# Reordering the gate steps and the removal counts in the first part of a two-layer graph kernel

## The chip, the cores and the metric

The kernel runs on one core of one Trainium2 chip. The metric is the device time in microseconds (us) of one execution, as the median of several. Engines: PE is TensorE, DVE is VectorE, ACT is ScalarE, POOL is GpSimd, SP is SyncE, which here only issues transfers. PEld is TensorE's loading of weights.

## The reference, cut to what matters

There are 16 graphs of 1024 nodes with 128 channels. Layer 0 is a gated graph network with four rounds; layer 1 first thins the neighbour lists of the same adjacency ("dilation"), row by row, and then runs three aggregating layers.

```python
# layer 0: x = layernorm(x + gated(x, adj))
for i in range(4):
    m = einsum('bjn,bjd->bnd', adj, h @ weight[i])
    gx, gh = m @ w_ih.T + b_ih, h @ w_hh.T + b_hh
    r = sigmoid(xr + hr); z = sigmoid(xz + hz); n = tanh(xn + r * hn)
    h = (1 - z) * n + z * h

# layer 1 begins with, for each graph, rows in order:
def step(carry, n):
    row = carry[n]; num = sum(row)
    sf = where(num > 10, (num + 1) // 2, 1)
    rank = cumsum(row)
    rm = row & (rank % sf == 0)        # if num > 1
    carry[n] &= ~rm; carry[:, n] &= ~rm
# ... three aggregating layers, a linear layer, layernorm
```

Both the four gated rounds and the thinning need only the inputs. The kernel runs them side by side: this is its first part, and the only one the change touches.

## The kernel before

**Gated rounds.** Two graphs are worked on at a time, each by a "stream". A layer of one stream is 32 products of the adjacency with h (h split in a high and a low half of its bits, two halves f of 512 nodes, 8 blocks j), then for each half f four gate sums and the gate steps. `aside(n)` is a hook: it advances the thinning by one step and does small jobs for the other stream, so that they lie between the products. This is the order in which each engine's queue is filled[...].

```python
    def layer(self, st, l, aside):
        ...
        for f in range(2):
            for n, part in enumerate((st.hi, st.lo)):
                aside(2 * f + n)
                if l == 0 and f == 1 and n == 0:
                    st.begin(1)
                for j in range(NB):
                    nc.tensor.matmul(pm[f], part[:, j, :], st.adj[j][:, half[f]], ...)   # L1074
            m = wk.tile([C, HF], F32, name="h_ms")
            nc.scalar.copy(m, pm[f])                                                     # L1077
            ms.append(m)
        aside(4)
        ...
        for f in range(2):
            h, m = st.ht[:, half[f]], ms[f]
            ...
            pr = gate((w(self.wh, 0), h), (w(self.wi, 0), m))                            # gate: L1086
            nc.scalar.activation(r, pr, AF.Sigmoid, bias=bias(self.bs, 0))               # L1095
            aside(5 + 2 * f)
            ph = gate((w(self.wh, 2), h))
            nc.vector.scalar_tensor_tensor(r, ph, bias(self.bh, 2), r, ...)              # L1098
            px = gate((w(self.wi, 2), m))
            nc.vector.tensor_add(r, px, r)                                               # L1100
            nc.scalar.activation(r, r, AF.Tanh, bias=bias(self.bi, 2))                   # L1101
            aside("rest" if f == 0 else 8)
            pz = gate((w(self.wh, 1), h), (w(self.wi, 1), m))
            nc.scalar.activation(z, pz, AF.Sigmoid, bias=bias(self.bs, 1))               # L1104

            nc.gpsimd.tensor_tensor(zh, z, h, ALU.mult)                                  # L1106
            nc.vector.scalar_tensor_tensor(r, z, 1.0, r, op0=ALU.subtract, op1=ALU.mult) # L1107
            nc.gpsimd.tensor_tensor(h, zh, r, ALU.subtract)                              # L1108
            aside(6 if f == 0 else 9)
```

The hook. In mid-graph its jobs are the "turn" of the other stream's new h (four transposes on PE, L1025), the copy of its high part ("split", ACT, L1013), and the low part ("rest", DVE, L1018), once for each half of h; the other stream's next products need them. Where the other stream ends or begins a graph, its jobs are the ending and beginning instead.

```python
            jobs = {5: [lambda: ot.next_layer(0)], "rest": [lambda: ot.rest(0)],
                    7: [lambda: ot.next_layer(1)], 8: [lambda: ot.rest(1)]}
        ...
        def aside(n):
            if n not in ("rest", 8):
                next(steps, None)
            for job in jobs.get(n, ()):
                job()
            if n == 8:
                next(steps, None)
```

**Thinning.** A block is 128 rows of four graphs, and there are 32 blocks. A block takes 20 steps, that is two layers (10 hooks each that advance it). Cut to the order of the work:

```python
            yield; old.settle(); old.wide_u(0)        # the block before: third counts, its rows
            yield; old.wide_u(1); old.rows(0)
            ...                                       # rows(g): DVE L863; wide_u: ACT L909, L912
            for g in range(4):                        # spread over the steps
                self.turn(i, g)                       # PE L722
                self.keep(i, a[g])                    # DVE L727
                self.count(i, g, a[g], rank, pt)      # DVE L735, a running count along the row
            q = self.params(num, 0)                   # DVE, some seven ops on 128x4
            u = self.diag_u(rank[:, :, diag], q)      # ACT L886, four
            yield
            x = self.removed(u, q, both)              # DVE L893, four: the removal mask
            yield; yield
            pd, num = self.less(x, rank, 1)           # PE L901, four, then DVE L903: second counts
            q = self.params(num, 1, ...)              # DVE L694 to L701, with L818
            u = self.diag_u(rd, q)                    # ACT L886, four
            yield
            x = self.removed(u, q, both)              # DVE L893
            yield; old = self.Block(self, i, a, rank, both, x)
```

`settle` is the third and last round: it starts with `less` (PE L901, DVE L903) and params again. With the offset of the start, the second round's counts fall on `aside(7)` of the first stream's layer, the second removal on its `aside(8)`, and `settle` on `aside(1)` of the second stream's layer.

Of the kernel before, what the change touches and what calls it, by code (L numbers as in the profile page):

```python
# [15 lines left out]
ALU = mybir.AluOpType  # L16
# [9 lines left out]
NB = N // P  # L26
HF = 512
L0 = 4
# [888 lines left out]
class Gated:  # L917
# [24 lines left out]
    def bank(self):  # L942
        return self.ps6.tile([P, HF], F32, name="h_g")
# [117 lines left out]
    def layer(self, st, l, aside):  # L1061

        nc, wk = self.nc, self.wk
        half = [slice(f * HF, (f + 1) * HF) for f in range(2)]
        bank = self.bank
        pm = [bank() for f in range(2)]
        ms = []
        for f in range(2):
            for n, part in enumerate((st.hi, st.lo)):
                aside(2 * f + n)  # L1070
                if l == 0 and f == 1 and n == 0:
                    st.begin(1)
                for j in range(NB):
                    nc.tensor.matmul(pm[f], part[:, j, :], st.adj[j][:, half[f]],  # L1074
                                     start=(j == 0 and n == 0), stop=(j == NB - 1 and n == 1))
            m = wk.tile([C, HF], F32, name="h_ms")
# [3 lines that stand above are left out]
        bias = lambda t, g: t[:, 3 * l + g:3 * l + g + 1]  # L1080
        w = lambda t, g: t[:, l, g, :]

        def gate(*mm):
            pg = bank()
            for i, (lhs, rhs) in enumerate(mm):
                nc.tensor.matmul(pg, lhs, rhs, start=(i == 0), stop=(i == len(mm) - 1))  # L1086
            return pg

        for f in range(2):
            h, m = st.ht[:, half[f]], ms[f]  # L1090
            r = wk.tile([C, HF], F32, name="h_r")
            z = wk.tile([C, HF], F32, name="h_z")
            zh = wk.tile([C, HF], F32, name="h_zh")
            pr = gate((w(self.wh, 0), h), (w(self.wi, 0), m))
# [3 lines that stand above are left out]
            nc.vector.scalar_tensor_tensor(r, ph, bias(self.bh, 2), r, op0=ALU.add, op1=ALU.mult)  # L1098
# [4 lines that stand above are left out]
            pz = gate((w(self.wh, 1), h), (w(self.wi, 1), m))  # L1103
            nc.scalar.activation(z, pz, AF.Sigmoid, bias=bias(self.bs, 1))  # L1104

            nc.gpsimd.tensor_tensor(zh, z, h, ALU.mult)  # L1106
            nc.vector.scalar_tensor_tensor(r, z, 1.0, r, op0=ALU.subtract, op1=ALU.mult)  # L1107
            nc.gpsimd.tensor_tensor(h, zh, r, ALU.subtract)  # L1108
            aside(6 if f == 0 else 9)

    def run(self, steps):

# [27 lines left out]
    def beside(self, st, ot, l, s, b0, steps):  # L1140


        before = l if s == 0 else l + 1
        if before in (0, L0):
            old = not (s == 0 and b0 == 0)
            new = not (s == 1 and b0 + 2 >= B)
            jobs = {5: [], 7: [], 9: []}
            nxt = ot.b + 2 if old else ot.b

            def begin():  # L1150
                ot.b = nxt
                ot.begin(0)

            if old:
                jobs[5].append(lambda: ot.finish(0))
                jobs[7].append(lambda: ot.finish(1))
                jobs[0] = [lambda: ot.load_x(nxt)]
                for j in range(4, NB):
                    jobs.setdefault(j // 2 - 2, []).append(lambda j=j: ot.load_adj(nxt, j))
            if new:  # L1160
                jobs.setdefault(5 if old else 0, []).append(lambda: ot.begin_rows(nxt))
                jobs[9].append(begin)
        else:
            jobs = {5: [lambda: ot.next_layer(0)], "rest": [lambda: ot.rest(0)],
                    7: [lambda: ot.next_layer(1)], 8: [lambda: ot.rest(1)]}

        if l == L0 - 1:

            for j in range(4):
                jobs.setdefault(4, []).append(lambda j=j: st.load_adj(st.b + 2, j))  # L1170

        def aside(n):
            if n not in ("rest", 8):
                next(steps, None)
            for job in jobs.get(n, ()):
                job()
            if n == 8:
                next(steps, None)
        return aside

# [809 lines left out]
```

## Time and profile before

| what | value |
|---|---|
| time, median of 3 | 2517.11 us (2514.15 to 2519.67) |
| profiled execution | 2516.4 us, 35661 instructions |
| first part | about 40 to 1417 us: 64 layers, 32 blocks |
| PE, DVE, ACT, POOL busy, share of the span | 91%, 76%, 55%, 41% |

The page has the span in 40 equal slices; each digit is the busy share of a slice in tenths.

```
PE   6999999999999999999999599999999989988875
DVE  4888888888878878888888777777777466665667
ACT  3556455556455564556564456666666445545647
```

The first 22 slices are the first part. DVE is busier there than anywhere later, ACT about half busy. [...]

### The profile page before, as it was taken

What the parts mean: (1) busy time and instruction counts of PE and PEld (TensorE: products, weight loads), DVE (VectorE), ACT (ScalarE), POOL (GpSimd) and SP (SyncE); (2) the same over time, 40 slices, a digit from 0 to 9 for tenths busy, and PEclk for the clock granted to TensorE, in tenths of its full rate; (3) what the DMA queues carried; (4) which work ended last, traced back from release to release, by engine and by line L of the source; (5) the groups of instructions that cost most, each with busy time, mean ns of one, the idle gap of its engine ahead of it and who ended that gap; (6) DMA issues with size and microseconds to landing.
All of it is one profiled execution on the core that took longest, in us unless ns stands there. A gap on an engine that the chain in (4) does not pass through costs nothing.

```text
span 2516.4 us, 35661 instructions
## 1 busy us (share of the span) xinstructions
PE 2287.6 (91%) x11897; PEld 1574.4 (63%) x11913; DVE 1925.0 (76%) x4153; ACT 1390.1 (55%) x3228; POOL 1035.2 (41%) x937
## 2 busy tenths in 40 slices
PE   6999999999999999999999599999999989988875
PEld 4556555555555565555555377777777777777654
DVE  4888888888878878888888777777777466665667
ACT  3556455556455564556564456666666445545647
POOL 3335234253353352442532376666666244440000
PEclk9999999999999999999999899999999999999988
DMA  7327245263363272443631487787777366655304
GB/s 248 106 91 248 68 141 179 88 216 109 103 213 106 92 248 68 149 171 102 216 100 60 141 305 271 280 294 289 283 278 260 135 218 235 232 167 157 118 16 130
DMA packets 214389, 436.17 MB, mean 173 GB/s; under 512 B 59570, under 2 KB 80724, under 8 KB 214196
## 3 DMA queue, kind: packets, MB, share of 16 engines
q1 hardware_dynamic: 186756, 345.96, 39.8%
q0 software_dynamic: 23040, 83.90, 9.8%
q10 hardware_dynamic: 4400, 3.95, 0.5%
q8 instruction: 96, 1.57, 0.3%
q14 instruction: 97, 0.79, 0.1%
HBM read 324.49 MB, written 109.25 MB: 172 GB/s over the span
## 4 chain that ended last, share of the span: by engine, by line
PE 42%; DVE 32%; ACT 15%; issue 6%; DMA 4%; POOL 1%; SPq 0%; DVEq 0%; ACTq 0%; POOLq 0%
PE p_ag L1531 9%; PE h_g L1074 8%; PE h_g L1086 7%; DVE f_rank L735 7%; DVE f_x L893 3%; DVE h_r L1107 3%; ACT f_pd L886 2%; ACT s_junk L1368 2%; PE q_ag L1764 2%; PE p_u L1458 2%; PE p_u L1459 2%; PE p_u L1452 2%; DVE f_a L727 2%; DVE h_r L1100 2%; DVE h_r L1098 2%
## 5 line engine op out<-in xcount | busy, mean ns | idle before, releaser
L1106 POOL TENSOR_TENSOR h_zh<-h_z,h_h 128x512 f32<-128x512 f32 x128 | 203.9, 1593 | 501.3 <-ACT h_z L1104 501.0
L1086 PE MATMUL h_g<-h_h,h_wh 128*128 128x512 f32 x768 | 397.8, 600 | 0.0
L1086 PE MATMUL h_g<-h_ms,h_wi 128*128 128x512 f32 x768 | 392.2, 592 | 0.0
L1074 PE MATMUL h_g<-h_a,h_hi 128*128 128x512 f32 x1024 | 289.7, 422 | 48.2 <-ACT h_hi L1013 48.2
L1467 POOL CAST p_b<-p_at 128x512 uint8<-128x512 f32 x256 | 256.4, 1021 | 129.7 <-ACT p_at L1460 129.7
L735 DVE TENSOR_TENSOR_SCAN f_rank<-f_a,f_first,f_pd 128x1024 f16<-128x1024 f32 x128 | 299.2, 2343 | 3.0
L1074 PE MATMUL h_g<-h_a,h_lo 128*128 128x512 f32 x1024 | 272.0, 410 | 0.0
L1460 ACT ACTIVATE p_at<-p_u,s_less 128x512 fp32r<-128x512 f32 x256 | 175.7, 688 | 156.9 <-PE p_u L1459 140.4
L1086 PEld LDWEIGHTS h_g<-h_ms,h_wi 128*128 128x128 f32 x768 | 145.8, 190 | 183.8 <-issue 164.9
L1074 PEld LDWEIGHTS h_g<-h_a,h_hi 128*128 128x128 f32 x1024 | 188.3, 190 | 114.7 <-ACT h_hi L1013 58.6
L1074 PEld LDWEIGHTS h_g<-h_a,h_lo 128*128 128x128 f32 x1024 | 201.2, 200 | 42.1
L863 DVE SCALAR_TENSOR_TENSOR f_nr<-f_u,f_q,f_a 128x1024 bf16<-128x1024 f16 x128 | 164.0, 1284 | 77.4 <-ACT f_u L912 68.1
L1476 DVE SCALAR_TENSOR_TENSOR p_a<-p_a 128x1024 bf16<-128x1024 f32 x128 | 210.5, 1685 | 3.7 <-DMA p_a<-in_adj_dram 3.7
L1101 ACT ACTIVATE h_r<-h_r,h_bi 128x512 f32<-128x512 f32 x128 | 92.6, 723 | 181.8 <-DVE h_r L1100 181.6
L1368 ACT ACTIVATE s_junk<-s_o 128x128 bf16<-128x128 f32 x384 | 113.7, 298 | 129.1 <-DVE s_o L1361 129.1
L1086 PEld LDWEIGHTS h_g<-h_h,h_wh 128*128 128x128 f32 x768 | 129.2, 191 | 82.4 <-issue 66.3
L1107 DVE SCALAR_TENSOR_TENSOR h_r<-h_z,h_r 128x512 f32<-128x512 f32 x128 | 114.1, 891 | 86.6 <-ACT h_z L1104 86.3
L1108 POOL TENSOR_TENSOR h_h<-h_zh,h_r 128x512 f32<-128x512 f32 x128 | 163.9, 1281 | 27.9 <-DVE f_tr L903 17.2
L909 ACT ACTIVATE f_u<-f_rank,f_q 128x128 f16<-128x128 f16 (+7 forms) x128 | 110.5, 866 | 89.2 <-DVE f_rank L849 89.2
L1077 ACT COPY h_ms<-h_g 128x512 f32<-128x512 f32 x128 | 73.8, 577 | 152.6 <-PE h_g L1074 111.1
L1458 PE MATMUL p_u<-ident_b,p_a 128*128 128x128 bf16 x1024 | 145.0, 222 | 5.1 <-DMA p_a<-in_adj_dram 4.1
L1459 PE MATMUL p_u<-ident_b,p_nr 128*128 128x128 bf16 x1024 | 144.9, 222 | 0.0
(242 smaller groups left out, 4899.4 us busy)
## 6 DMA issues: line engine op xcount, KB each, us to landing
h_a<-in_adj_dram POOLq DMA_DIRECT2D x128, 512.0 KB, 7.2
p_a<-in_adj_dram SPq DMA_DIRECT2D x128, 512.0 KB
f_a<-in_adj_dram SPq DMA_DIRECT2D x124, 512.0 KB
e_nr<-f_nr SPq DMA_DIRECT2D x128, 256.0 KB
p_nr<-e_nr SPq DMA_DIRECT2D x32, 1024.0 KB
s_at<-p_b SPq DMA_DIRECT2D x32, 512.0 KB
s_ag<-s_ag SPq DMA_DIRECT2D x64, 256.0 KB
q_agi<-s_ag SPq DMA_DIRECT2D x32, 512.0 KB
```

The costliest lines, as they stand in the source:

```text
L735: nc.vector.tensor_tensor_scan(out, a, other[:, 0, 0:1].to_broadcast([P, N]), start, op0=ALU.add, op1=ALU.bypass)
L1074: nc.tensor.matmul(pm[f], part[:, j, :], st.adj[j][:, half[f]], start=(j == 0 and n == 0), stop=(j == NB - 1 and n == 1))
L1086: nc.tensor.matmul(pg, lhs, rhs, start=(i == 0), stop=(i == len(mm) - 1))
L1106: nc.gpsimd.tensor_tensor(zh, z, h, ALU.mult)
L1107: nc.vector.scalar_tensor_tensor(r, z, 1.0, r, op0=ALU.subtract, op1=ALU.mult)
L1368: self.nc.scalar.activation(junk, o[:, i, :], AF.Square, accum_out=ss[:, i:i + 1])
L1458: nc.tensor.matmul(pu[:, i * P:(i + 1) * P], a[:, blk, 1], ib, start=False, stop=False)
L1459: nc.tensor.matmul(pu[:, i * P:(i + 1) * P], nr[:, k, blk], ib, start=False, stop=(i == 3))
L1460: nc.scalar.activation(g["at"][:, j, cols], pu, AF.Relu, bias=self.less2)
L1467: self.nc.gpsimd.tensor_copy(g["b", f][:, j, :], g["at"][:, j, f * HF:(f + 1) * HF].bitcast(F32))
L1476: self.nc.vector.scalar_tensor_tensor(low, a, 0.0, a, op0=ALU.is_gt, op1=ALU.not_equal, accum_out=self.bad[:, c:c + 1])
L1531: self.nc.tensor.matmul(pa, hi[:, j, :], at[:, j, f * HF:(f + 1) * HF], start=(start and n == 0), stop=(stop and n == len(js) - 1))
```

## The change

Three things change in the order of instructions; none is added or left out.

1. In `aside(7)` of layers whose other stream is in mid-graph, the turn and split of h's second half come before the step of the thinning (second counts, their parameters, L886).
2. The last two gate steps of the first half (L1107 and L1108) are put off until both halves' gates are emitted. They thereby come behind the steps at `aside(7)` and `aside(8)`: the second counts and the second removal in the first stream's layer, the masking of row 1 in the second's. The second half's L1106 now stands behind the first half's L1108 on GpSimd.
3. `aside(1)`, with the third counts of the block before, moves from ahead of the low products of the first half to between the fourth and the fifth of them.

They are meant to let the products and the thinning wait less for each other. Lines of the changed kernel are up to 12 higher than those of before.

```diff
@@ layer: products
             for n, part in enumerate((st.hi, st.lo)):
-                aside(2 * f + n)
+                if (f, n) != (0, 1):
+                    aside(2 * f + n)
                 if l == 0 and f == 1 and n == 0:
                     st.begin(1)
                 for j in range(NB):
+                    if (f, n, j) == (0, 1, NB // 2):
+                        aside(1)
                     nc.tensor.matmul(pm[f], part[:, j, :], st.adj[j][:, half[f]],
@@ layer: gates
+        rest = []
         for f in range(2):
             h, m = st.ht[:, half[f]], ms[f]
...
             pz = gate((w(self.wh, 1), h), (w(self.wi, 1), m))
             nc.scalar.activation(z, pz, AF.Sigmoid, bias=bias(self.bs, 1))
 
-            nc.gpsimd.tensor_tensor(zh, z, h, ALU.mult)
+            rest.append((r, z, zh, h))
+            if f == 0:
+                nc.gpsimd.tensor_tensor(zh, z, h, ALU.mult)
+                aside(6)
+        for f, (r, z, zh, h) in enumerate(rest):
+            if f == 1:
+                nc.gpsimd.tensor_tensor(zh, z, h, ALU.mult)
             nc.vector.scalar_tensor_tensor(r, z, 1.0, r, op0=ALU.subtract, op1=ALU.mult)
             nc.gpsimd.tensor_tensor(h, zh, r, ALU.subtract)
-            aside(6 if f == 0 else 9)
+        aside(9)
@@ beside: the hook
         def aside(n):
-            if n not in ("rest", 8):
+
+            first = n == 7 and before not in (0, L0)
+            if not first and n not in ("rest", 8):
                 next(steps, None)
             for job in jobs.get(n, ()):
                 job()
-            if n == 8:
+            if first or n == 8:
                 next(steps, None)
         return aside
```

## The prediction

> **What bounds the kernel now.** I read the page's busy line first, then the busy times by stretch, then the waits of TensorE and VectorE in the first part, and last the timeline of one period.
>
> ```profile
> PE 2287.6 (91%) x11897; PEld 1574.4 (63%) x11913; DVE 1925.0 (76%) x4153; ACT 1390.1 (55%) x3228; POOL 1035.2 (41%) x937
> 40.00:1417.00 1377.00, 1292.27 (x5029) 786.42 (x5027) 1151.03 (x2214) 764.13 (x1410) 543.86 (x485) 0.98 0.41 136
> ```
>
> The second line is the first part, the only one that the change touches (span, then busy time of PE, PE loads, DVE, ACT, POOL). TensorE idles 1377.0 - 1292.3 = 84.7 us there. The part holds 64 gated layers, alternately of two streams. The row-removal search takes 20 steps for a block of rows and a layer calls 10, so layers pair up: in A (first stream) the search counts rows 2 and 3 and does its first and second removal, in B (second stream) it settles the third count, writes the rows and counts rows 0 and 1 of the next block. There are 32 pairs, of 1377/32 = 43.0 us.
>
> ```profile
> PE h_g L1074 <- ACT h_hi L1013: 48.2, 24, 2.1
> PE f_pd L901 <- DVE f_x L893: 32.8, 44, 1.9
> ```
>
> These two waits (total, times, longest) are 81.0 of the 84.7 us. The first is the product that wants the split of h's second half, once in each of the 24 pairs in which the other stream is in mid-graph; the second is a count of removals waiting for VectorE's removal mask.
>
> ```profile
> DVE h_r L1107 <- ACT h_z L1104: 86.3, 90, 2.9
> DVE f_nr L863 <- ACT f_u L912: 68.1, 92, 1.2
> ```
>
> VectorE, in turn, loses most of its waiting to L1107, the last gate step, which stands in its queue before its z is there. The timeline at the A-to-B seam shows what that does (start, duration, engine and line):
>
> ```profile
> 827.56 0.68 DVE L1018 TENSOR_TENSOR h_lo<-h_g,h_hi 128x512 fp32r<-128x512 f32 x1
> 829.00 0.69 DVE L1107 SCALAR_TENSOR_TENSOR h_r<-h_z,h_r 128x512 f32<-128x512 f32 x1 [0.77 <-ACT h_z L1104]
> 829.62 0.16 DVE L903 TENSOR_TENSOR f_tr<-f_rank,f_pd 128x4 f32<-128x4 f16 x1
> ...
> 831.06 1.95 ACT L886 ACTIVATE f_pd<-f_rd,f_q 128x128 f32<-128x128 f16 x4 [1.51 <-DVE f_t L700]
> 832.95 0.58 ACT L1013 CAST h_hi<-h_g 128x512 fp32r<-128x512 f32 x1
> 833.55 0.69 DVE L1018 TENSOR_TENSOR h_lo<-h_g,h_hi 128x512 fp32r<-128x512 f32 x1 [0.84 <-ACT h_hi L1013]
> 833.58 1.21 PE L1074 MATMUL h_g<-h_a,h_hi 128*128 128x512 f32 x4 [2.05 <-ACT h_hi L1013]
> 834.16 1.12 DVE L893 SCALAR_TENSOR_TENSOR f_x<-f_pd,f_q,f_both 128x128 bf16<-128x128 f32 x4
> 834.79 1.27 POOL L1106 TENSOR_TENSOR h_zh<-h_z,h_h 128x512 f32<-128x512 f32 x1 [2.61 <-ACT h_z L1104]
> 835.20 1.42 DVE L1107 SCALAR_TENSOR_TENSOR h_r<-h_z,h_r 128x512 f32<-128x512 f32 x1
> 835.34 0.40 PE L901 MATMUL f_pd<-f_tri,f_x 128*128 128x128 bf16 x4 [0.56 <-DVE f_x L893]
> 836.54 0.15 DVE L903 TENSOR_TENSOR f_tr<-f_rank,f_pd 128x4 f32<-128x4 f16 x1
> ```
>
> L1107 holds up the second round's parameters (L903 on); these hold up ScalarE's L886; L886 stands before the split (L1013) in ScalarE's queue; the split holds up the product and lo; lo holds up the mask; the mask the third count. The loop that sets the period is thus the search itself, on VectorE and ScalarE, round to the next block; TensorE waits where it meets it. That is my choice of bound, and it matters: shortening only TensorE's waits would move them elsewhere.
>
> [...] the split starts at 832.95, behind L886, though the turn it reads was issued at 826.46 and ran 0.61 us. [...] L1107 at 835.20 takes 1.42 us, ending 0.56 after GpSimd's L1106 ended at 836.06, against 0.69 undisturbed. [...] here six banks rotate, and in the built program the turn of the second half waits for the bank that the first half's r sigmoid reads. This bears on a rival below.
>
> **The change, part by part**, on the pair above. No instruction is added or dropped; only places in queues move. R is the end of L1100 of the first half in A, at 827.64.
>
> Turn before counts, and L1107 put off, in A. Lo of the first half ends at 828.24. L903 then follows at about 828.28 instead of 829.62, 1.34 earlier (0.77 of wait and 0.69 of work gone, less overlap). L700, whose end releases ScalarE, ends at 829.69 instead of 831.03. The second half's r sigmoid ends at 829.56 (828.88 + 0.68), and the split now follows it: 829.56 to 830.14. The product that waited needs it after four products, about 831.0: the 2.05 us wait is gone. L886 runs 830.1 to 832.05. Meanwhile VectorE does L1098, L1100 and lo of the second half, until about 832.0, and the mask (1.12) ends at 833.2 instead of 835.28: 2.06 earlier.
>
> Third count four products on. TensorE starts its products at 830.01, eight take about 1.9 us, four more 0.9: it reaches the count at 832.8, at the mask's arrival but for 0.4 us. Before, it would have stood still from 832.0. VectorE now does both L1107 (2 x 0.69), 833.2 to 834.6, and goes on with L903 at 834.6 instead of 836.54: 1.94 earlier.
>
> B. The rows (L863) are paced by ScalarE's L909/L912, which start 1.94 earlier too; the last row ends about 2.0 earlier. Then the block's own mask (L774), L1098, L1100 and lo as before; L1107 of the first half with its wait (0.77 + 0.69) no longer stands before row 0's masking and count, so these come 2.0 + 1.46 - 0.1 = 3.3 earlier. It comes back behind row 1's masking, with 0.69 and without the 0.31 us that the second half's L1107 waited there: 3.3 - 0.69 + 0.31 = 2.9 earlier from there to the next R.
>
> So the search's loop shortens by about 2.8 us a pair. In the eight pairs in which the turn is not moved (a graph ends or begins there), L1107 waited 2.90 us in the one at 744.15; there ScalarE becomes free for L886 only 2.1 earlier, and L903 of the settling gains about 1.9, so these gain as much. 32 x 2.8 = 90 us. TensorE cannot give that much: its idle time is 84.7 us in all, plus small holds inside runs of matmuls (a 0.50 us load wait at 827.70). On the pair above, 42.39 us from third count to third count (835.34 to 877.73), I take off its waits of 2.05, 0.56 and 0.26 and about 0.5 of load waits: 39.0 us of pure TensorE. The loop would come to 42.4 - 2.8 = 39.6. Two lengths so close do not interlock without loss; I keep 75%: 32 x 2.8 x 0.75 = 67 us. The end of the part costs about 1.5 us: after the last layer h's first half is ready only behind the second half's gates, and GpSimd does its three steps one after another (1.27 each). 2517 - 67 + 1.5, rounded down a little for the contention that L1107 loses (mean 891 ns against 690; 128 x 0.2 = 26 us of VectorE, a part on the loop): 2449 us.
>
> **Rivals.** (1) TensorE is the bound and its wait only moves, to the first round's count, where 16 pairs already wait 0.2 to 1.5 us for the mask. Against it: these masks come from the same loop, which is shortened. For it: if ScalarE rather than VectorE paced B, the 0.9 of gain in B would be lost, leaving 1.94 x 32 x 0.75 = 47 us: 2470. (2) GpSimd's three steps now run back to back after the mask, from 834.6 to about 838.4 (3 x 1.27), into the first row at 837.6, which reads two SBUF tiles and would stand still some 0.8 us. For it: the 1.42 us above. Against: later rows wait 0.6 us each for ScalarE, and swallow it. If they did not: 32 x 0.8 x 0.75 = 19 us less, 2468. (3) The turn, now ahead of the second round's count, waits for its bank: in the heavy pair at 1044 the r sigmoid ends at 1043.98 and the mask at 1044.60, so turn and count would fall together. The count would come up to 0.5 us later in perhaps 16 pairs: 6 to 8 us, 2456. (4) [...] granted 0.98 here; one point over the part would be 14 us.
>
> **Range and chances.** All three losses together would still leave some 25 us of gain; full interlock would give 80 to 90. I take 2430 to 2473 for 8 in 10. The line of 2% is 2466.8, which rivals 1 and 2 would each just miss: faster 0.77, same 0.22, slower 0.01.
>
> **What would show it.** Right: L1074's wait on L1013 gone from TensorE's list; L1107's wait on L1104 far under 86 us; the period from third count to third count near 40.9; TensorE's idle time in the part under 35 us. Rival 1: waits of L901 on L893 at the first round's count grow beyond 20 us. Rival 2: L863's mean rises above 1284 ns. Rival 3: the turn (L1025) appears waiting for L1095. I am wrong if the period shrinks by under 1.5 us, above all if row 0's count does not come about 3 us earlier after the seam.

## The result, and the profile after

The changed kernel takes 2426.2 us (median of five, 2424.7 to 2427.8) against 2517.0 us (2514.2 to 2519.7) for the kernel before: a ratio of 0.964, 95% interval 0.9627 to 0.9654. That is 91 us less. I had predicted 2449 us, 2430 to 2473: the direction was right, the gain was a third larger than said, and the result lies just below the range.

The busy line of the page after, and the busy times of the first part, which now ends near 1323 us instead of 1417 (span, then PE, PE loads, DVE, ACT, POOL, granted clock of TensorE, share of the DMA engines, GB/s):

```profile
PE 2260.7 (93%) x11897; PEld 1558.2 (64%) x11913; DVE 1927.9 (80%) x4153; ACT 1384.0 (57%) x3228; POOL 1014.2 (42%) x937
40.00:1323.00 1283.00, 1264.46 (x5014) 770.62 (x5013) 1148.60 (x2209) 755.79 (x1407) 516.51 (x482) 1.00 0.43 145
```

TensorE idles 18.5 us of the part, where it idled 84.7. But 66 us less idling is not 91 us less time: over the whole kernel TensorE is also busy 27 us less (2260.7 for 2287.6), with the same 11897 products, and its granted clock in the part rose from 0.98 to 1.00. The waits of TensorE in the part (total, times, longest):

```profile
PE h_g L1077 <- DMA h_a<-in_adj_dram: 7.4, 12, 1.4
PE h_g L1037 <- ACT h_z L1108: 4.5, 5, 1.2
PE h_g L1089 <- DVE h_r L1102: 3.5, 13, 0.3
PE h_g L1025 <- ACT h_r L1099: 2.8, 7, 0.5
```

Both waits that made up the idle time before, of the product for the split and of the count for the mask, are gone from the list. What leads it now is new: products that wait for a block of the adjacency. Three of VectorE's waits in the same part (those left out are of 6.4 us and less):

```profile
DVE f_nr L863 <- ACT f_u L912: 50.4, 69, 1.2
DVE h_r L1102 <- ACT h_r L1099: 21.4, 9, 3.6
DVE h_r L1117 <- ACT h_z L1108: 3.7, 7, 0.5
```

L1117 is L1107 of before; its wait fell from 86.3 to 3.7 us. The timeline of the seam that the prediction worked through, in the kernel after, cut to the steps that it named:

```profile
775.63 0.68 DVE L1018 TENSOR_TENSOR h_lo<-h_g,h_hi 128x512 fp32r<-128x512 f32 x1
776.23 0.16 DVE L903 TENSOR_TENSOR f_tr<-f_rank,f_pd 128x4 f32<-128x4 f16 x1
777.52 0.58 ACT L1013 CAST h_hi<-h_g 128x512 fp32r<-128x512 f32 x1
777.98 1.97 ACT L886 ACTIVATE f_pd<-f_rd,f_q 128x128 f32<-128x128 f16 x4
778.35 2.41 PE L1077 MATMUL h_g<-h_a,h_hi 128*128 128x512 f32 x8
779.99 1.13 DVE L893 SCALAR_TENSOR_TENSOR f_x<-f_pd,f_q,f_both 128x128 bf16<-128x128 f32 x4
780.60 1.08 PE L1077 MATMUL h_g<-h_a,h_lo 128*128 128x512 f32 x4
781.03 1.29 DVE L1117 SCALAR_TENSOR_TENSOR h_r<-h_z,h_r 128x512 f32<-128x512 f32 x2
781.52 0.40 PE L901 MATMUL f_pd<-f_tri,f_x 128*128 128x128 bf16 x4
781.88 1.58 POOL L1118 TENSOR_TENSOR h_h<-h_zh,h_r 128x512 f32<-128x512 f32 x1 [3.48 <-DVE h_r L1117]
```

L903 follows lo at once. The split (L1013) now starts ahead of L886 (777.52 and 777.98; before, L886 started at 831.06 and the split at 832.95, the order of ScalarE's queue in each), so eight products run in one piece where one stood 2.05 us. From the end of lo (776.31) to the end of the mask (781.12) it is 4.8 us, 7.0 before: 2.2 earlier, where the prediction said 2.06. Products and count follow on TensorE without a wait.

The pairs do not share alike in this. Below are the busy times of three pairs, each from third count to third count: one with an early block of its graphs, which takes over the removals of few blocks ahead of it (light), one with a late block (heavy), and one in which a graph ends and the next begins. Before:

```profile
490.20:532.58 42.38, 39.55 (x152) 23.68 (x153) 36.37 (x72) 22.53 (x40) 14.54 (x14) 1.00 0.42 134
576.02:620.12 44.10, 40.66 (x165) 24.52 (x165) 36.87 (x72) 24.45 (x44) 14.80 (x12) 1.00 0.31 99
708.76:750.05 41.29, 39.42 (x152) 24.57 (x152) 32.28 (x61) 25.64 (x53) 28.90 (x32) 1.00 0.78 267
```

The same three after:

```profile
457.73:496.57 38.84, 38.84 (x153) 23.83 (x153) 35.92 (x72) 22.43 (x40) 13.54 (x13) 1.00 0.44 146
539.20:580.21 41.01, 40.29 (x165) 24.60 (x165) 36.98 (x72) 23.93 (x44) 13.70 (x11) 1.00 0.34 106
661.71:703.54 41.83, 40.19 (x153) 24.34 (x153) 34.14 (x62) 25.81 (x54) 29.29 (x32) 1.00 0.77 264
```

Over all pairs: twelve light ones fell from 42.6 to 38.9 us, twelve heavy ones from 44.4 to 40.7, and the pairs with a change of graph went from 42.2 to 42.5 (seven of the eight lie between two third counts). So 24 pairs gained 3.7 us each and those with a change of graph gained nothing; the prediction gave all 32 the same 2.8. In the light pair TensorE is busy for the whole of its 38.84 us. That number is its floor, and the light pairs stand on it.

### The profile page after: what moved, and what is told of

It reads as the page before. It is cut to its first block, busy times and chain, and to the rows that moved or that the text cites. A ratio compares the mean times of both kernels' runs of the same rounds, so it can differ in the third digit from the quotient of the medians.

```text
span 2423.1 us, 35665 instructions
## 1 busy us (share of the span) xinstructions
PE 2260.7 (93%) x11897; PEld 1558.2 (64%) x11913; DVE 1927.9 (80%) x4153; ACT 1384.0 (57%) x3228; POOL 1014.2 (42%) x937
## 3 DMA queue, kind: packets, MB, share of 16 engines
q1 hardware_dynamic: 186756, 345.96, 41.5%
## 4 chain that ended last, share of the span: by engine, by line
PE 49%; DVE 22%; ACT 12%; DMA 8%; issue 6%; POOL 3%; SPq 0%; DVEq 0%; ACTq 0%; POOLq 0%
PE h_g L1089 12%; PE p_ag L1543 9%; PE h_g L1077 9%; DVE f_rank L735 4%; DMA e_sum<-h_x 3%; ACT s_junk L1380 2%; PE q_ag L1776 2%; PE p_u L1470 2%; PE p_u L1471 2%; PE p_u L1464 2%; ACT f_u L909 2%; DMA h_a<-in_adj_dram 2%; DVE f_x L893 2%; PE q_ob L1740 2%; PE s_tr L1402 1%
## 5 line engine op out<-in xcount | busy, mean ns | idle before, releaser
L1077 PE MATMUL h_g<-h_a,h_hi 128*128 128x512 f32 x1024 | 284.0, 417 | 7.5 <-DMA h_a<-in_adj_dram 7.4
L1118 POOL TENSOR_TENSOR h_h<-h_zh,h_r 128x512 f32<-128x512 f32 x128 | 184.7, 1443 | 198.1 <-DVE h_r L1117 170.7
L1077 PE MATMUL h_g<-h_a,h_lo 128*128 128x512 f32 x1024 | 262.0, 393 | 0.0
L863 DVE SCALAR_TENSOR_TENSOR f_nr<-f_u,f_q,f_a 128x1024 bf16<-128x1024 f16 x128 | 183.8, 1453 | 57.1 <-ACT f_u L912 50.4
L1112 POOL TENSOR_TENSOR h_zh<-h_z,h_h 128x512 f32<-128x512 f32 x64 | 81.6, 1275 | 323.7 <-ACT h_z L1108 323.7
L1077 PEld LDWEIGHTS h_g<-h_a,h_lo 128*128 128x128 f32 x1024 | 189.9, 188 | 38.3
L1740 PE MATMUL q_ob<-s_wxp,q_xt 128*128 128x256 f32 x512 | 130.8, 399 | 0.0
```

What stands on the lines that cost most here:

```text
L863: nc.vector.scalar_tensor_tensor(nr, self.us[g], self.q[:, 2, g:g + 1], self.a[g], op0=ALU.not_equal, op1=ALU.is_ge)
L1740: nc.tensor.matmul(pb[:, i], g["xt"][:, f, blk], self.wxp, start=False, stop=(i % 2 == 1))
```

## The experiments

Three questions were open: what each part is worth and which loop it shortens; where the 27 us of TensorE's busy time went; and what holds the pairs with a change of graph. The theory of the prediction is called loop (the search on VectorE and ScalarE sets the period), its rival TensorE (TensorE's waits set it). Each ratio is to the kernel before, timed on the same chip. Kernels whose names hold dve, four_more or fill have work added whose results are thrown away or rewritten as they were.

### Each part alone, and in pairs

**turn** is the kernel before with only the hook changed.

```diff
+            first = n == 7 and before not in (0, L0)
+            if not first and n not in ("rest", 8):
-            if n not in ("rest", 8):
                 next(steps, None)
...
-            if n == 8:
+            if first or n == 8:
                 next(steps, None)
```

> Only part 1 of the change (turn and split ahead of the second counts). Loop theory: the split no longer stands behind L886, so the mask comes about 1.1 us earlier in 24 pairs, 26 us in all, near 2491 us (2483 to 2500); TensorE's wait moves from L1074 to the third counts L901, about 2 us each, and half-clock stretches remain. TensorE theory: the 48 us of L1074's wait are gained, and clock with them: 2469 us or below.

Measured: 2490.5 us, ratio 0.988 (0.986 to 0.990). Loop is right. The wait on the split is gone, and this came in its place:

```profile
PE f_pd L901 <- DVE f_x L893: 58.0, 33, 2.7
```

Nearly all of it, 57.7 us, is at the third counts, where it was 23.2 before: of the 48.2 us for which TensorE stood for the split, 34.5 came back here. Its wait was a place where it met the loop, not the loop.

**late** puts only the last gate steps of the first half off.

```diff
-            nc.gpsimd.tensor_tensor(zh, z, h, ALU.mult)
+            rest.append((r, z, zh, h))
...
-            aside(6 if f == 0 else 9)
+        aside(9)
```

> Only part 2 (first half's L1107 and L1108 put off). Loop theory: parameters start 1.3 us earlier in A, row 0's masking 1.4 earlier in B and 0.4 of that is kept, about 2.0 us a pair: near 2453 us (2443 to 2465), L1074's wait falls to about 0.7 to 1.0 us each, and half-clock stretches become few. TensorE theory: the split is still behind L886 and the third count still in its old place, so at most 30 us: 2487 us or above.

Measured: 2452.8 us, ratio 0.973 (0.972 to 0.975), as loop had it, though this edit touches neither the turn nor a product. It is nearly three quarters of the whole gain (66 of 91 us). The two waits of TensorE remain, but none is longer than 0.6 us.

**four** moves only the third counts four products on.

```diff
-                aside(2 * f + n)
+                if (f, n) != (0, 1):
+                    aside(2 * f + n)
...
+                    if (f, n, j) == (0, 1, NB // 2):
+                        aside(1)
```

> Only part 3 (third counts behind four low products). Loop theory: the mask's time does not change and TensorE comes to the count when the mask is there: 2517 us within 5, the wait of L901 at this place gone, that of L1074 unchanged at 48 us. TensorE theory: about 20 us of L901's wait gained, 2497 us.

Measured: 2515.0 us, ratio 0.9986 (0.9979 to 0.9993): next to nothing alone, though TensorE's wait at the third counts fell from 23.2 to 5.1 us. At the second counts it grew from 11.8 to 18.1 us. Room for a count is worth nothing while the mask sets when the count can start.

The pairs of parts, put together from these edits: **turn_late**, **turn_four** and **late_four**.

> Parts 1 and 2 without part 3 (third counts back ahead of the low products). Loop theory with TensorE now as long as the loop: TensorE reaches the count about 1.2 us before the mask, and what it loses there it cannot make up: waits of L901 near 1 us in each of 32 pairs, 2445 us (2437 to 2455). If the loop alone still set the period, place 3 would be worth nothing: 2426 to 2430 us. If part 3 is worth only what it was by itself: 2430 us.

> Parts 1 and 3 without part 2. Loop theory: without part 2 the loop is as long as with part 1 alone: 2487 us (2480 to 2492), TensorE waiting at the third counts for less (about 1.5 us each instead of 2). TensorE theory: part 3 takes off 0.9 us in 32 pairs: 2461 us.

> Parts 2 and 3 without part 1 (split again behind L886). Loop theory: the mask comes about 0.8 us later than in the changed kernel in 24 pairs, 20 us at most: 2440 us (2432 to 2448); L1074's wait on the split about 0.5 us, 24 times. If the parts simply add: 2449 us. If part 1 has nothing left to give: 2426 us.

Measured: 2433.2, 2473.3 and 2445.5 us, ratios 0.966 (0.965 to 0.968), 0.982 (0.980 to 0.984) and 0.971 (0.969 to 0.973). late_four came within its range. turn_late and turn_four were 12 and 14 us faster than expected; turn_four thereby lies midway between the two theories (2487 and 2461). In turn_late the count waits 16.1 us in all, at most 0.7, half of what was expected. In turn_four the count's wait is at most 1.7 us where it was 2.7 in turn, and with it something else vanished, the next subject: the light pairs that had none of it in turn (41.0 us in the mean) are as long as those of turn_four (40.9).

### TensorE's clock

In the records of the kernel before, TensorE's granted clock is not evenly 0.98: it is 1.00, but for 13 stretches of half clock of some 3.4 us each. One of them, in busy times by steps of 2 us (columns as above; the clock is the third number from the right):

```profile
874.00:876.00 2.00, 0.03 (x1) 0.04 (x1) 1.05 (x3) 1.93 (x5) 0.57 (x1) 1.00 0.00 0
876.00:878.00 2.00, 1.44 (x7) 0.92 (x8) 2.00 (x6) 1.11 (x2) 0.81 (x1) 0.81 0.00 0
878.00:880.00 2.00, 2.00 (x9) 1.61 (x7) 1.93 (x7) 0.00 (x0) 1.28 (x2) 0.50 0.03 8
880.00:882.00 2.00, 2.00 (x9) 1.65 (x8) 0.97 (x6) 1.70 (x3) 2.00 (x4) 0.84 0.00 0
```

TensorE waits 2.05 us for the split, does four products, waits 0.56 us for the mask, and then runs at half clock, which costs 1.7 us of clock a time: 22 us in all, most of the 27 us of busy time. The same two waits at the seam of the prediction, at 833 us, were followed by none. In the clock records of this trace each of the 13 stretches lasts 3.41 us, and all begin on one grid of 3.413 us: from the first, at 143.38 us, to the last, at 1351.69, it is 354 steps. Here are the windows of that grid with the first wait at 833 us, which was not followed by half clock, and with the one at 874 us, which was:

```profile
829.46:832.87 3.41, 2.07 (x7) 0.94 (x5) 3.04 (x11) 1.80 (x5) 2.64 (x2) 1.00 0.00 0
873.83:877.24 3.41, 1.29 (x5) 0.67 (x4) 2.46 (x6) 3.18 (x7) 0.80 (x2) 1.00 0.00 0
```

TensorE is idle for 1.34 us of the first window, since an edge of the grid (832.87) cuts the wait in two, and for 2.12 us of the second, which holds the wait whole. So it is throughout this trace: in the 13 windows ahead of a stretch TensorE is idle for 1.88 to 2.23 us, in every other window of the part for 1.71 or less. The first part of the kernel after has no such stretch, and in its windows, laid on the grid of its own later stretches, TensorE is idle for 1.19 us at most. turn has 10 stretches and four about 10 (granted clock over the whole execution 0.975 and 0.973, where the kernel before has 0.971 and the kernel after 0.980), and late, turn_four, turn_late and late_four have none (0.980, 0.979, 0.979 and 0.979). These are counts from one trace each; whether anything but the waits lowers the clock was not tried.

**before_fill** gives the kernel before eight products at the wait for the split, so that TensorE is not idle there; their result is overwritten.

```diff
+                    if st.s == 1 and l > 0 and (f, n, j) == (0, 0, NB // 2):
+                        for i in range(8):
+                            nc.tensor.matmul(pm[1], part[:, i % 4, :], st.adj[i % 4][:, half[0]],
+                                             start=True, stop=True)
```

> The kernel before with eight more products (their sums are thrown away) in the place of L1074's wait in 24 layers, some 1.9 us each, so that TensorE stands still less than 1 us at a time. If the half-clock stretches (22 us of lost clock in the profile of before) cost time: granted clock in the part 1.00 instead of 0.98 and 2497 to 2510 us in spite of 192 added products. If the loop's slack hides them: clock 1.00 and 2517 us within 5. If the clock does not follow the waits: clock 0.98, and 2517 us or more.

Measured: 2508.7 us, ratio 0.996 (0.995 to 0.998). With 192 products more, the kernel is 10 us faster, and no stretch of half clock is left in its first part. So the clock was worth about 10 us of time, half of the 22 us of clock; the rest must have lain where the search's loop was the longer, which no run separates.

### What the loop and TensorE can bear

Work was added to one engine at a time, before and after: **before_dve** and **after_dve** run L818 twice (0.68 us of VectorE a pair), **before_four_more** and **after_four_more** have four products more a pair (0.9 us of TensorE).

```diff
-            q = self.params(num, 1, lambda: nc.vector.tensor_sub(rd, rank[:, :, diag], pd))
+            q = self.params(num, 1, lambda: [nc.vector.tensor_sub(rd, rank[:, :, diag], pd) for _ in range(2)])
```

```diff
+                    if st.s == 1 and (f, n, j) == (1, 0, 0):
+                        for i in range(4):
+                            nc.tensor.matmul(pm[1], part[:, i, :], st.adj[i][:, half[1]],
+                                             start=True, stop=True)
```

> The kernel before with L818 done twice (the same result written again), 0.68 us more on VectorE in each of 32 blocks, ahead of L886. Loop theory: all of it is on the loop, +20 us: 2538 us (2532 to 2544). If TensorE sets the period: 2517 to 2521 us.

> The changed kernel with the same doubling of L818. If the loop still sets the period: +20 us, 2446 us. If TensorE does, with slack left in the loop: 2426 to 2430 us. As the two lengths are held to be close, about half: 2436 us (2430 to 2442).

> The kernel before with four more products a pair on TensorE (sums thrown away), ahead of the second half's products of the second stream, 0.22 us each, 28 us in all. Loop theory: they take the place of waits; 2519 us (2514 to 2524). If TensorE sets the period: 2545 us.

> The changed kernel with the same four products more a pair. TensorE is busy for 98.6% of the first part there, so they should cost nearly all of their 28 us: 2451 us (2444 to 2456). If the loop set the period: 2426 to 2431 us.

Measured, in the same order: 2545.7 (ratio 1.011, 1.010 to 1.013), 2437.2 (0.968, 0.967 to 0.970), 2539.6 (1.009, 1.008 to 1.011) and 2438.3 us (0.969, 0.967 to 0.970).

Before, 22 us of VectorE cost 28: the two pairs all but free of half clock in both traces grew by the full 0.7 (41.3 to 42.0, 40.5 to 41.2), and there were 24 stretches of half clock instead of 13 (granted clock over the execution 0.964 for 0.971). VectorE is on the loop. After, the same 22 us cost 11: heavy pairs grew by 0.6 in the mean, light ones by 0.3, where TensorE's floor had left the loop some slack. The four products missed the expected 2519 by 21 us, and the reason is again the clock: pairs without a stretch kept their length (42.8 and 42.8, 44.1 and 44.1), pairs that took one on grew by 1.8 (42.4 to 44.2), and there were 19 stretches (granted clock 0.969). So TensorE before had room for four products, but not for four at half clock. After, four products cost 12 us for 28 us of work: light pairs grew by the full 0.9 (38.7 to 39.6), heavy ones by 0.0 to 0.4. So in the kernel after the light pairs are held by TensorE and the heavy ones by the search.

### The place of one GpSimd step

In the kernel after, L1106 of the second half stands behind L1108 of the first on GpSimd. My rival 2 took that for a harm. **early_zh** is the kernel after with this one step back at its earlier place.

```diff
+            nc.gpsimd.tensor_tensor(zh, z, h, ALU.mult)
             if f == 0:
-                nc.gpsimd.tensor_tensor(zh, z, h, ALU.mult)
                 aside(6)
...
-            if f == 1:
-                nc.gpsimd.tensor_tensor(zh, z, h, ALU.mult)
```

> The changed kernel with the second half's L1106 issued to GpSimd before the first half's L1108, so that GpSimd is done about 1.3 us earlier and the first row (L863) does not meet it. Mean of L863 from 1453 ns back to about 1300. If TensorE sets the period of the changed kernel: 2426 us within 4. If the loop does: about 0.5 us in 32 pairs, 2410 us.

Measured: 2460.7 us, ratio 0.978 (0.976 to 0.979): 34 us slower than the kernel after. The groups of the last gate step (count, busy time and mean ns, then idle time before it), first in the kernel after:

```profile
L1117 DVE SCALAR_TENSOR_TENSOR h_r<-h_z,h_r 128x512 f32<-128x512 f32 x128 | 98.6, 805 | 3.7 <-ACT h_z L1108 3.7
```

and in early_zh:

```profile
L1115 DVE SCALAR_TENSOR_TENSOR h_r<-h_z,h_r 128x512 f32<-128x512 f32 x128 | 151.8, 1218 | 4.1 <-ACT h_z L1108 3.6
```

The step takes 53 us more of VectorE, 1218 ns in the mean for 805, and all that changed is the place of L1106 in GpSimd's queue. L863 became shorter in return (mean 1338 against 1453 ns), as rival 2 had it, but part of that comes back as waiting: its wait for L912 is 60.3 us here and 50.4 in the kernel after. The place behind L1108 is no harm but a good part of what makes the put-off pay.

### The pairs with a change of graph

These gained nothing, and in the kernel after three things stand out there: the load of the next graph's x waits for the store of the old graph's sum (54.5 us on GpSimd, 25.9 before), with ScalarE's split of x behind it (24.6 us, 2.3 before); GpSimd makes lo of x with two subtractions in a row; and TensorE waits for the adjacency. Each was taken away or cut down.

**after_x7** and **before_x7** hold x as half tiles, seven of them instead of three whole ones, loaded and stored by halves; h_w keeps one buffer. **after_x7_turn** also lets the turn precede the second counts in these pairs (`first = n == 7`).

```diff
-                self.x[b] = self.top.wk.tile([P, NB, C], F32, name="h_x", bufs=3)
-                self.nc.gpsimd.dma_start(self.x[b], rows_of(self.top.x[b]))
+                self.x[b] = [self.top.wk.tile([P, 4, C], F32, name="h_x", bufs=7) for f in range(2)]
+                for f in range(2):
+                    self.nc.gpsimd.dma_start(self.x[b][f], rows_of(self.top.x[b])[:, 4 * f:4 * f + 4, :])
...
```

> The kernel after the change, with a graph's x held as two tiles of half its rows each, seven of them instead of three whole ones (paid for by one h_w tile), each half loaded and stored by itself, so that the next graph's x does not wait for the store of the sum of the graph that ended. Theory W (in the eight pairs with a change of graph the gain is lost to that wait: GpSimd's load L1009 stands 8 us behind the store, ScalarE's split of x L1044 24.6 us in all behind the load, and the gates and removals behind the split): both waits gone, these pairs 0.8 to 1.5 us shorter, 2414 to 2419 us. Theory T (these pairs were near TensorE's own length already: 40.8 us of matmuls in 42.2 before, 40.8 in 42.5 after, and the rest is waits for the adjacency): waits gone, pairs shorter by under 0.4 us, 2423 to 2427 us.

> The same halves of x in the kernel before the change, where ScalarE's split of x waits for the load 2.3 us in all. Both theories: 2513 to 2518 us.

> As after_x7, and the turn of the second half precedes the second round's counts in the pairs with a change of graph too. Theory L (the unmoved turn holds these pairs up as it did the others): another 0.5 to 1 us in each of eight pairs, 4 to 8 us less than after_x7. Theory T: within 2 us of after_x7, or longer by the 1.1 us that the mask on the turn (L1055) takes of ScalarE ahead of the parameters' L886, 8 us more.

Measured: 2432.5 us (ratio 0.967, 0.965 to 0.968), 2564.3 (1.019, 1.018 to 1.020) and 2435.4 (0.967, 0.966 to 0.969). For ScalarE's wait theory W fell: it went from 24.6 to 2.8 us, and the pairs are no shorter (43.4 us). GpSimd's wait for the store was only halved (28.9 of 54.5 us), so that this part of the theory is not settled here. Half clock is a part of the 43.4 us: three of the seven pairs hold a stretch (44.5 us each); the four without take 42.6, where the same four take 42.2 in the kernel after. Theory L fell with it: the earlier turn gains nothing either (44.2 us, 42.7 in the two without a stretch). The waits of TensorE in the first part of after_x7 begin:

```profile
PE h_g L1079 <- DMA h_a<-in_adj_dram: 16.1, 13, 1.9
```

The wait for the adjacency doubled, from 7.4 us: TensorE no longer waits for the turn of x (4.5 us in the kernel after), and waits there instead.

That before_x7 would be 47 us slower was in no expectation. Of this, 44 us lie in the seven pairs with a change of graph (42.2 to 48.5 us in the mean). The timeline shows what is new there, first in the kernel before:

```profile
200.25 2.95 POOL L1045 TENSOR_TENSOR h_lo<-h_x,h_hi 128x512 fp32r<-128x512 f32 x2
201.20 0.87 DVE L1107 SCALAR_TENSOR_TENSOR h_r<-h_z,h_r 128x512 f32<-128x512 f32 x1 [1.81 <-ACT h_z L1104]
```

and in before_x7:

```profile
199.22 4.27 DVE L1109 SCALAR_TENSOR_TENSOR h_r<-h_z,h_r 128x512 f32<-128x512 f32 x1 [1.82 <-ACT h_z L1106]
199.23 2.49 POOL L1046 TENSOR_TENSOR h_lo<-h_x,h_hi 128x512 fp32r<-128x512 f32 x2
201.68 1.26 POOL L1108 TENSOR_TENSOR h_zh<-h_z,h_h 128x512 f32<-128x512 f32 x1
```

Before, the gate step, begun 0.95 us after the first of GpSimd's two subtractions, ended 1.13 us ahead of the end of the second. With a store issued ahead of them (0.59 us) both engines begin together, and VectorE's step ends only 0.55 us after the third of three GpSimd steps. Fourteen steps of 4.0 us or more stand in this trace, two in each of the seven pairs, and none of 2 us in the trace of before; the gate step's mean over the kernel goes from 891 to 1248 ns, some 46 us of VectorE. That is the size of the loss, but no run took these collisions out of before_x7, and it also has 24 stretches of half clock instead of 13 (granted clock 0.964 for 0.971).

**after_x7_no_lo** and **after_no_lo** leave these two subtractions out from the third graph on.

```diff
+                if b < 2:
-                self.nc.gpsimd.tensor_tensor(self.lo[:, rows, :], x[f],
+                    self.nc.gpsimd.tensor_tensor(self.lo[:, rows, :], x[f],
```

> after_x7 without the two subtractions on GpSimd (L1046, 1.27 us each, one behind the other) that make lo of a new graph's x, from the third graph on: it leaves that part of the computation out. Theory P (with the wait for x gone, the last gate step on VectorE, 1607 ns in the mean of one such pair and up to 5.75 us for one, stands behind these subtractions; that and nothing else holds the pairs with a change of graph at 43.4 us): the pairs come down to TensorE's own 41 to 41.5 us, 14 to 19 us in seven or eight pairs, 2412 to 2419 us. Theory T (they are held by TensorE and the adjacency's arrival): 2428 to 2433 us.

> The kernel after the change without the same two subtractions, the wait of the next graph's x for the store of the old sum left in. Theory P with the wait as a second cause (either alone keeps the pair long): pairs with a change of graph from 42.5 to about 41.8 us, 2419 to 2424 us. If the wait costs nothing once the subtractions are gone: as after_x7_no_lo, 2412 to 2418 us. Theory T: 2424 to 2427 us.

Measured: 2433.7 us (ratio 0.967, 0.965 to 0.969) and 2426.7 (0.9635, 0.962 to 0.965), as after_x7 and as the kernel after. Theory P fell too. The collision is there (gate steps of up to 5.75 us in after_x7, of 3.2 us in the kernel after), and taking these two subtractions out gains nothing in these kernels, since something else is later.

**after_no_adj** is the kernel after without the loads of the adjacency for the gates from the third graph on; the gates go on with that of the first two, so the transfer is left out and the number of products is the same.

```diff
         def load_adj(self, b, j):
-            if b < B:
+            if b < 2:
```

> The kernel after the change, in which the gate part loads no adjacency from the third graph on and computes on with that of the first two: it leaves this part of the work out. Theory D (in the pairs with a change of graph TensorE's 40.8 us of matmuls and its waits for the new adjacency, 7.4 us in seven pairs beside 4.5 us for the turn of x, are what is left, so that neither the wait for x nor the collision on GpSimd could give anything): waits for h_a gone, these pairs from 42.5 to 40.8 to 41.3 us, 9 to 14 us in all, 2412 to 2418 us. Theory S (the search's loop holds these pairs and TensorE only waits where it meets it): another wait comes in place of the adjacency's, pairs within 0.4 us of 42.5, 2423 to 2427 us.

Measured: 2406.0 us, ratio 0.956 (0.954 to 0.957), 20 us faster than the kernel after. The pair with a change of graph, the same one as above:

```profile
652.84:692.12 39.28, 39.28 (x154) 24.56 (x153) 33.88 (x63) 27.18 (x55) 24.64 (x21) 1.00 0.35 121
```

41.83 us became 39.28, all of it TensorE; the seven pairs came from 42.5 to 39.8 us with no idle time of TensorE left. Theory D is right in kind, and the gain was larger than it said (9 to 14): of 2.7 us a pair, 1.7 had been idle time of TensorE and 1.0 had counted as busy. The light pairs stayed at 38.8, the heavy ones at 40.6. So the loads of the next graph's adjacency, or what comes with them, hold these pairs, and the search does not. The run takes away the whole of them: the arrival, GpSimd's issuing (6.4 us in the pair above) and the traffic, and with them went ScalarE's wait for x, GpSimd's wait for the store, and the gate steps of over 2 us. ScalarE's wait and the long steps are no rivals, since after_x7_no_lo cut both and gained nothing. GpSimd's wait is one, with four adjacency loads behind it in the queue: after_x7_no_lo left 44.7 of its 54.5 us.

Whether the blocks come late for want of a free buffer or for want of transfer was not tried, but the trace of the kernel after tells for this pair. From 667.43 us on GpSimd issued seven loads in a row without a wait, and an eighth waited 1.22 us for its buffer. Then the DMA engines were full (the share 1.10, 404 GB/s):

```profile
672.00:688.00 16.00, 14.63 (x58) 9.56 (x57) 15.57 (x12) 7.59 (x18) 11.84 (x11) 1.00 1.10 404
```

The load that the pair's critical chain goes through was issued at 669.01 us and landed 12.7 us later, where the median load takes 7.4. TensorE waited 1.37 us for it, and 0.28 us for one of the four loads that stand behind the wait for the store. So in this pair it was mostly transfer, and neither a buffer nor the store; whether loads issued earlier would help stays open.

## Why the prediction was right or wrong

**The bound.** Right. turn, late, four and before_dve all came out as the loop had it and not as TensorE's waits had it; turn_four and before_four_more came between the two, and the difference lies in the pairs with half clock, whose cost neither theory counted. The two waits that the prediction adds up to "81.0 of the 84.7 us" are 83.2 us over the window of the 84.7 (the second is 35.0 us, 45 times). TensorE's length without its waits, put at 39.0 us on a light pair, is 38.84.

**The steps of the seam.** Right in kind and nearly in size. The mask came 2.2 us earlier for 2.06; the settling's L903 starts 782.23 - 776.31 = 5.9 us after lo, where it was 836.54 - 828.24 = 8.3, so 2.4 earlier for 1.94. The wait at L1117 is 3.7 us for 86.3. That 0.4 us passes on to what follows, and the loop would then be about 3.2 us shorter instead of 2.8. The heavy pairs, which the search held before and holds after, show it whole: 44.3 us at full clock (before_fill) became 40.7, so 3.6 shorter; in the light pair it is at least 3.54 (42.38 to 38.84). The last few tenths are not traced to a step.

**"Two lengths so close do not interlock without loss; I keep 75%".** This is the step that failed. There was no such loss: the light pairs have TensorE's length (38.86 us in the mean, TensorE idle for 0.02 of them), the heavy ones the loop's (40.7, TensorE idle for 0.5). Without the factor the sum stood at 90 us, and 91 was measured.

**"so these gain as much".** The other failed step, in the opposite direction, and hidden by the first in the total. The pairs with a change of graph did not become 2.8 us shorter but 0.3 longer, and 1.0 longer if half clock is left aside (41.5 in before_fill, 42.5 after). The step looked only at VectorE and ScalarE. Without the adjacency's loads these pairs take 39.8 us, so the search allows that much; but the loads, or what comes with them, set the end, and no line of the prediction asked when they land. Why they end later than before is open, since the kernel before was not run without these loads. The agreement of 90 with 91 is thus in part luck: 24 x 3.7 = 89, less 7 x 0.3 = 2, make 87, and the rest lies at the ends.

**What the range lacked.** Two terms were missing that add to the gain of the 24 pairs. One is the clock. Rival 4 counted it as a loss; with the long waits gone TensorE got 1.00 in the part instead of 0.98, and the term is about +10 us by before_fill. The other is the gate step's contention, for which I rounded down: its mean fell from 891 to 805 ns, since the put-off brings L1106 of the second half behind it (1218 ns with L1106 ahead, in early_zh).

**The end of the part.** "about 1.5 us" was too pessimistic: the last turn's wait for GpSimd, 8.6 us before, is 6.5 in two waits after.

**The rivals.** Rival 1 (the wait moves to the first round's count, which the plan of the thinning calls the second counts): not so in the whole change, where no wait of L901 is left, nor in turn, where it moved to the third counts. Only in four alone did it grow there, from 11.8 to 18.1 us. Rival 2 (three GpSimd steps run into the first row): L863's mean did rise, from 1284 to 1453 ns, but early_zh shows that the same order saves 34 us. Rival 3 (the turn waits for its bank): there, with 2.8 us in seven waits, of no weight.

## What to carry to other kernels

When two loops interlock, work out the length of each and take the longer; a flat discount for "interlocking" is a guess that no view supports, while the pairs of periods that differ in kind (here those with new transfers) each need their own answer to what ends last. Look at the granted clock in fine steps before calling it an average: here some waits of 2.05 us were followed by half clock that took another 1.7 us of clock, and added work or a cleared wait changed the number of such stretches along with what it was meant to change. And count the order in GpSimd's queue as much a part of a change as the order in VectorE's: here the place of one GpSimd step made 34 us (early_zh).

## What the runs showed of the hardware that was not expected

- Half clock after short waits: in the first part of the trace of before, each window of a fixed grid of 3.413 us in which TensorE was idle for 1.88 us or more was followed by one at 0.5, 13 in all, and none with 1.71 us or less was. Eight useless products in the wait made the kernel 10 us faster.
- The last gate step on VectorE, 0.69 us at 829.00 in the kernel before, took 4.27 us in before_x7 when it began together with a run of three GpSimd steps of about 1.25 us each, and ended 0.55 us after the third. In the kernel before, begun 0.95 us after the first of two such steps, it took 0.87 us. What sets the order of the two engines, these traces do not show.
- Leaving out 14 graphs' adjacency loads for the gates gave 20 us, although the waits of TensorE that name them were only 7.4 us in all. Of the 2.7 us in each of the seven pairs, 1.7 had been idle time of TensorE under all names and 1.0 had counted as busy.
